# Output projections of four attention layers: seven block products, a bias on the scalar engine, and one batch of x kept in DRAM

## The chip, the core and the metric

The kernel runs on one core of a Trainium2 chip. It is one launch, and the metric is the device time of that launch in microseconds (us), as the median of three runs. A separate execution was recorded by the hardware profiler; all rows below come from it. Engines are named as in the profile: PE is TensorE (matrix products), PEld its weight loads, DVE is VectorE, ACT is ScalarE, POOL is GpSimd, and SP is the engine whose queue issues the DMAs. [...]

## The reference

Four layers in float32, one after the other, on `x` of 4 batches, 512 channels and 1024 positions. Every layer adds its result to `x`. Cut to what matters:

```python
# layer 0: attention with 8 heads of 64; layer 3: the same with 4 heads of 128, on group-normalised x
qkv = xs @ Wp.T + bp
attn = softmax(q @ k.T * SCALE)
res = attn @ v                      # heads side by side: 512 channels
out = res @ Wo.T + bo + xs          # the output projection, and x added

# layer 1: linear attention without a softmax, x + gamma * wval
# layer 2: attention with one head of 512 on layer-normalised x, x + out
```

## The kernel before

Channels are split into `NC` = 4 chunks of 128, so a batch of x is a tile of 128 partitions, 4 chunks and 1024 positions: 16 KB in each partition, 2 MB in all. The four batches stay in on-chip memory for the whole program (`xs`, line 559). Positions are split into two blocks of `TB` = 512. Layers 0 and 1 are interleaved: the linear attention of batch b - 1 (layer 1) is cut into `pieces`, which are put between the products of the query, key and value projection of batch b (layer 0). Then layer 2 runs over all batches, then layer 3. `plain_path` is the path that is timed. A general path behind it runs only when the largest sums of exponentials pass a limit.

**Seven products.** `seven_products` (line 685 to 800) computes a product of two-by-two blocks with seven block products and some additions in place of eight. The block sums of inputs are made by VectorE (`sum_inputs`, lines 665 to 668, four passes), those of weights by GpSimd (`sum_weights`, lines 673 to 676). The projections of queries, keys and values use it with 512 moving columns (L685) or 256 (`weights_moving`, L801). Before the change the output projection does not.

**Attention** (`attention`, for layers 0 and 3) is a loop over steps: two blocks of queries (`qb`), four groups of channels (`g`), and 8 steps of keys in layer 0 (a group there is a pair of heads) or 4 in layer 3. A step issues `scores` (products into one of two score buffers, an exponential of 128x1024 on ScalarE at L891, and a running sum on VectorE at L895 and L898) and, two steps later, `values` (L910 or L925). After a group's last step `sum_rows` sums the exponentials over partitions on TensorE (L937 or L945), VectorE takes the reciprocal (L657), and `normalise` (L954) multiplies the group's result into its chunk of `ot`. The exponentials have four buffers.

**The output projection** (`project_out`) of a block of queries needs all four chunks of `ot`. It is put on the list `later` with a count, and `tick`, called in every step, lets it run when the count is spent: in layer 0 five steps after its block's last one, in layer 3 three. The second block's projection falls into the next batch's query and key projection, where `seven_products` calls what is left on the list after its sixth call. It is 16 products of 128x512 (L969), and VectorE then adds result and bias to x:

```python
xv = x[:, o, bass.ts(qb, TB)]
nc.vector.scalar_tensor_tensor(xv, ps, bo[:, o : o + 1], xv, ALU.add, ALU.add)   # L958
```

In layer 3 each of the results then goes to the output by a DMA. The last block of the whole program has a projection of its own (`end_program`, L982 and L989).

**PSUM.** Products accumulate in `acc` tiles of 512 columns (`ps_acc`, 4 of them, a bank each) and score tiles of two banks (`ps_sc`, 2). In layer 0 a running group holds two `acc` tiles, one for each half of the partitions of the keys; in layer 3 it holds one.

**Order.** TensorE's instructions stay in the order in which the code issues them (`tc.manual_schedule`). Those of the other engines are ordered by a scheduler when the program is built, and `tc.issue_after` pins a few.

Of the kernel before, what the change touches and what calls it, by code (L numbers as in the profile page):

```python
# [13 lines left out]
F32 = mybir.dt.float32  # L14
# [460 lines left out]
def plain_path(ctx: ExitStack, tc: tile.TileContext, d: dict, out: bass.AP, count):  # L475
# [6 lines left out]

    nc = tc.nc

    const = ctx.enter_context(tc.tile_pool(name="const", bufs=1))
# [2 lines left out]
    work = ctx.enter_context(tc.tile_pool(name="work", bufs=1))  # L490
    small = ctx.enter_context(tc.tile_pool(name="small", bufs=2))
    PSUM = bass.MemoryType.PSUM
    ps_acc = ctx.enter_context(tc.tile_pool(name="ps_acc", bufs=4, space=PSUM))
    ps_sc = ctx.enter_context(tc.tile_pool(name="ps_sc", bufs=2, space=PSUM))

    def acc_tile():
        return ps_acc.tile([P, TB], F32, tag="acc", name="acc")
# [58 lines left out]
            nc.vector.tensor_tensor(bo, bo, cols[:, COL[name] : COL[name] + NC], ALU.add)  # L556
        return bo

    xs = [xpool.tile([P, NC, S], F32, tag=f"x{b}", name=f"x{b}") for b in range(B)]
# [5 lines left out]
    wview = d["wqkv0"].rearrange("(c p) o -> p c o", p=P)  # L565
    for c in range(NC):
        nc.sync.dma_start(xs[0][:, c, :TB], xin[0, :, c, :TB])
        nc.sync.dma_start(wqkv0[:, c, :C], wview[:, c, :C])
# [120 lines left out]
    def seven_products(  # L689
        n, weights, inputs, bias, dst, sums, ws=None, matmul=tokens_moving, view=lambda ps: ps,  # L690
        slots=0, first=False, done=lambda tb, o: None,
    ):

        stt = nc.vector.scalar_tensor_tensor
        one, five, seven, made = {}, {}, {}, {}
        inner = lambda o: block_sums(lambda i, j: weights(i, j, o))

        def mult(o, ps, w, x, start=True, stop=True, ms=(0, 1)):
            for m in ms:
                matmul(ps, w, x, m, o, start and m == 0, stop and m == 1)

        def join(out, ps, i, o, other):

            if bias is None:
                nc.vector.tensor_tensor(out, view(ps), other, ALU.add)  # L714
            else:
                joined[:] = [stt(out, view(ps), bias(i, o), other, ALU.add, ALU.add).ins]

        def p1(o, ms=(0, 1)):
            if 0 in ms:
                one[o] = acc_tile()  # L720
            mult(o, one[o], weights(0, 0, o), inputs(0, 0), stop=False, ms=ms)
            if 1 in ms:
                nc.scalar.copy(dst(0, 1, o), view(one[o]))

        def p2(o, ms=(0, 1)):
            mult(o, one[o], weights(0, 1, o), inputs(1, 0), start=False, ms=ms)
            if 1 in ms and bias is None:
                nc.scalar.copy(dst(0, 0, o), view(one.pop(o)))
            elif 1 in ms:
                nc.scalar.activation(dst(0, 0, o), one.pop(o), AF.Identity, bias=bias(0, o))  # L730

        def p3(o):
            mult(o, five[o], made[o][3], inputs(1, 1), start=False)
# [24 lines left out]
        if first:  # L758
            for f in (p1, p2):
                for m in range(2):  # L760
                    for o in range(n):
                        f(o, (m,))
            for o in range(2):
                made[o] = inner(o)
            t = sums()
        else:
            calls = [(p1, 0), (p1, 1), (p2, 0), (p2, 1)]
            if n > 2:
                calls += [(p1, 2), (p1, 3), (p2, 2), (p2, 3)]
# [88 lines left out]
        project_v(vt, wv, inputs, made, room())  # L858
        return q, k

    def attention(b, q, key, v, heads, scale, wo, bo, hooks={}, last=False, end=None):

# [86 lines left out]
        def normalise(qb, g):  # L949
            rd = rds.pop((qb, g))  # L950
            if g == 0 and not pair:
                ots[qb] = chunks_tile("ot", "ot")
            o = ots[qb][:, g, :]
            nc.vector.tensor_tensor(o, o if pair else outs.pop((qb, g))[0], rd, ALU.mult)  # L954

        def finish(qb, o, ps):
            xv = x[:, o, bass.ts(qb, TB)]
            nc.vector.scalar_tensor_tensor(xv, ps, bo[:, o : o + 1], xv, ALU.add, ALU.add)  # L958
            if last:
                nc.sync.dma_start(xout[b, :, o, bass.ts(qb, TB)], xv)  # L960

        def project_out(qb):
            ot = ots.pop(qb)

            for a in range(0, NC, 2):
                two = {o: acc_tile() for o in (a, a + 1)}
                for cs in (range(NC - 1), (NC - 1,)):
                    for o, c in itertools.product(two, cs):
                        nc.tensor.matmul(  # L969
                            two[o], lhsT=wo[:, c, bass.ts(o, P)], rhs=ot[:, c, :],  # L970
                            start=(c == 0), stop=(c == NC - 1),
                        )
                for o, ps in two.items():
                    finish(qb, o, ps)
# [24 lines left out]
        for m in range(0, len(steps) + 2, per):  # L999
# [3 lines left out]
            for n in range(m, m + per):  # L1003
                if n >= 2:
# [11 lines left out]
                    if n - 2 == len(steps) - 1 and end is not None:  # L1016
                        flush()
                        end_program(qb)
                    elif final and g == NC - 1:
# [341 lines left out]
    with tc.manual_schedule(engines={mybir.EngineType.PE}):  # L1361
# [8 lines left out]
        for b in range(B):  # L1370
# [12 lines left out]
            attention(b, q, lambda c, j: k[:, c, bass.ts(j, P)], vt, 8, 64.0**-0.5, wo0, bo0[0])  # L1383

# [59 lines left out]
        for b in range(B):  # L1444
# [28 lines left out]
            if b == 0:  # L1473

                query_sums()
            if b + 1 < B:
                norms = [layer_norm(b + 1, tb, after) for tb in range(NTB)]
                (add0, *n0), (add1, *n1) = norms
# [5 lines left out]
            else:  # L1484
# [29 lines left out]
        for b in range(B):  # L1514
# [6 lines left out]
            )  # L1521
            if b == 0:
                wo3 = load_wo(d["wo3"])
            flush()
            hooks = {}
            if b + 1 < B:
                ready = {}
# [2 lines left out]
                        lambda tb=tb, ready=ready: group_normed(b + 1, tb, ready)  # L1530
                    )
            attention(
                b, q, lambda c, j: k[:, c, bass.ts(j, P)], vt, 4, 128.0**-0.5, wo3, bo3, hooks,
                True, verdict if b == B - 1 else None,
            )

# [66 lines left out]
```

## Time and profile before

| quantity | value |
|---|---|
| median of 3 runs | 2527.16 us (2525.58 to 2527.5) |
| the profiled execution's own time | 2526.19 us |
| its span | 2524.3 us |
| mean granted TensorE clock | 0.999 |
| ScalarE busy | 657.2 us, 26% of the span |
| GpSimd busy | 239.0 us, 9% |
| L969, output projections: records, busy | 480, 211.7 us |
| L958, result and bias added to x: count, mean | 60, 751 ns |
| L898, running sum in attention: count, mean | 256, 1224 ns |
| L657, reciprocals in layers 0 and 3: count, mean | 64, 3358 and 3353 ns |
| one load of a whole batch of x, 2 MB: median from issue to landing | 20.8 us (three queued together) |

How to read it: the span is the profiled execution from its first to its last instruction, and its own time is 1.9 us more. A row of a timeline has its start, its length, the engine, the line of the kernel, the operation, output and input with shapes, and how many instructions it joins; in brackets stands the idle time of the engine just before it, and what ended that. A float32 matrix product leaves two records. The busy times of overlapping matrix products are modelled, so their lengths are better read from the chain of waits, where a row has start, length and the number of records.

### The profile page before, as it was taken

Reading aid. Unit: us, or ns where it says so; the run is one execution under the profiler, and the core shown is the slowest. Engines: PE = TensorE matmul, PEld = TensorE weight load, DVE = VectorE, ACT = ScalarE, POOL = GpSimd, SP = SyncE. Lnnn points to the kernel's source line nnn. Section 1 sums busy time; section 2 is a strip of 40 time slices with the busy share of each in tenths; the row PEclk is TensorE's granted clock in tenths of the full one; section 3 lists DMA queues with packets and bytes.
Section 4 is the critical chain, followed back from the end, with each engine's and each line's share of the span. In section 5 each row is a group of like instructions: output and inputs, shape, how many; then the busy total and the mean of one; then the engine's idle time right before and its main releaser. Section 6 shows DMA issues by size and latency. Waiting matters only on the chain.

```text
span 2524.3 us, 23992 instructions
## 1 busy us (share of the span) xinstructions
PE 2508.8 (99%) x9930; PEld 1245.0 (49%) x9930; DVE 1530.1 (61%) x1689; ACT 657.2 (26%) x781; POOL 239.0 (9%) x232
## 2 busy tenths in 40 slices
PE   9999999999999999999999999999999999999999
PEld 4544544454445444644646446445446445544643
DVE  3787588658865888657374563635643663654455
ACT  1443154315431643121110201012211220221121
POOL 3001100110020002002103011020010001002000
PEclk9999999999999999999999999999999999999999
DMA  6000000000000101000000000100000000000000
GB/s 246 1 1 1 5 1 1 1 5 1 1 1 14 50 9 42 5 1 0 0 1 1 0 4 1 67 0 17 17 17 1 0 17 17 1 17 17 1 13 22
DMA packets 17412, 38.87 MB, mean 15 GB/s; under 512 B 1552, under 2 KB 2064, under 8 KB 17296
## 3 DMA queue, kind: packets, MB, share of 16 engines
q1 hardware_dynamic: 17296, 37.26, 4.2%
q8 instruction: 80, 1.31, 0.2%
q14 instruction: 36, 0.29, 0.0%
HBM read 27.82 MB, written 8.39 MB: 14 GB/s over the span
## 4 chain that ended last, share of the span: by engine, by line
PE 98%; DVE 1%; DMA 0%; ACT 0%; issue 0%; SPq 0%; DVEq 0%; ACTq 0%
PE acc L685 19%; PE acc L801 12%; PE acc L1068 9%; PE acc L925 9%; PE sc L887 9%; PE acc L910 9%; PE sc L882 9%; PE acc L969 8%; PE acc L808 7%; PE acc L937 1%; PE acc L945 1%; PE feat L622 1%; PE acc L622 1%; PE acc L1160 1%; PE xt L1131 1%; PE upd L1226 1%
## 5 line engine op out<-in xcount | busy, mean ns | idle before, releaser
L891 ACT ACTIVATE pt<-sc 128x1024 f32<-128x1024 f32 x384 | 379.9, 1022 | 692.8 <-PE sc L887 408.5
L898 DVE TENSOR_TENSOR sum<-sum,pt 128x1024 f32<-128x1024 f32 x256 | 313.2, 1224 | 50.0 <-ACT pt L891 36.7
L910 PE MATMUL acc<-pt,v 64*64 64x512 f32 x2048 | 290.8, 590 | 0.0
L882 PE MATMUL sc<-q,k 64*64 64x512 f32 x2048 | 275.0, 590 | 1.1 <-ACT pt L891 1.1
L887 PE MATMUL sc<-q,k 128*128 128x512 f32 x512 | 240.0, 593 | 0.7 <-ACT pt L891 0.7
L925 PE MATMUL acc<-pt,v 128*128 128x512 f32 x512 | 239.9, 592 | 0.0
L969 PE MATMUL acc<-ot,wo 128*128 128x512 f32 x480 | 211.7, 595 | 0.8 <-DVE ot L954 0.8
L673 POOL TENSOR_TENSOR ws<-wqkv 128x256 f32<-128x256 f32 (+1 forms) x40 | 40.8, 1020 | 1417.4 <-PE acc L937 550.3
L657 DVE RECIPROCAL rd<-acc 128x512 f32<-128x512 f32 x32 | 107.5, 3358 | 109.7 <-PE acc L945 109.7
L685 PE MATMUL acc<-t,ws 128*128 128x512 f32 x384 | 173.9, 593 | 0.0
L1068 PE MATMUL acc<-pt,v 128*128 128x512 f32 x384 | 170.2, 592 | 0.0
L910 PEld LDWEIGHTS acc<-pt,v 64*64 64x64 f32 x2048 | 110.9, 133 | 112.7 <-issue 77.3
L882 PEld LDWEIGHTS sc<-q,k 64*64 64x64 f32 x2048 | 107.2, 133 | 116.0 <-issue 75.0
L925 PEld LDWEIGHTS acc<-pt,v 128*128 128x128 f32 x512 | 97.3, 190 | 122.5 <-issue 121.5
L887 PEld LDWEIGHTS sc<-q,k 128*128 128x128 f32 x512 | 96.7, 190 | 119.0 <-issue 97.5
L969 PEld LDWEIGHTS acc<-ot,wo 128*128 128x128 f32 x480 | 90.0, 190 | 120.6 <-issue 110.6
L958 DVE SCALAR_TENSOR_TENSOR x<-acc,bo,x 128x512 f32<-128x512 f32 x60 | 45.1, 751 | 146.5 <-PE acc L969 143.3
L1068 PEld LDWEIGHTS acc<-pt,v 128*128 128x128 f32 x384 | 72.8, 190 | 90.9 <-issue 89.2
L685 PEld LDWEIGHTS acc<-t,ws 128*128 128x128 f32 x384 | 72.5, 190 | 89.2 <-issue 87.5
L657 DVE RECIPROCAL rd<-rs 128x512 f32<-128x512 f32 x32 | 107.3, 3353 | 1.1
L895 DVE TENSOR_TENSOR sum<-pt 128x1024 f32<-128x1024 f32 x64 | 76.5, 1196 | 45.7 <-ACT pt L891 45.7
L714 DVE TENSOR_TENSOR v<-acc,v 128x512 f32<-128x512 f32 x72 | 49.7, 691 | 65.9 <-PE acc L801 65.7
(252 smaller groups left out, 3144.9 us busy)
## 6 DMA issues: line engine op xcount, KB each, us to landing
out<-x SPq DMA_DIRECT2D x32, 256.0 KB, 2.0
x<-in_x SPq DMA_DIRECT2D x3, 2048.0 KB, 20.8
wo<-in_wo SPq DMA_DIRECT2D x3, 1024.0 KB, 5.1
w<-in_w SPq DMA_DIRECT2D x1, 3072.0 KB, 11.1
wqkv<-in_wqkv SPq DMA_DIRECT2D x1, 3072.0 KB, 10.1
wqkv<-in_wqkv SPq DMA_DIRECT2D x2, 1024.0 KB, 10.0
x<-in_x SPq DMA_DIRECT2D x4, 256.0 KB, 4.9
wqkv<-in_wqkv SPq DMA_DIRECT2D x4, 256.0 KB, 5.4
```

The source lines that it names most:

```text
L657: nc.vector.reciprocal(rd, ps)
L685: nc.tensor.matmul(ps, lhsT=w[:, m, :], rhs=x[:, m, :], start=start, stop=stop, skip_group_check=True)
L801: nc.tensor.matmul(ps[:, bass.ts(r, C // 2)], lhsT=x[:, m, bass.ts(2 * o + r, P)], rhs=w[:, m, :], start=(start and r == 0), stop=stop, sk ...
L808: nc.tensor.matmul(ps, lhsT=x[:, m, bass.ts(o, P)], rhs=w[:, m, :], start=start, stop=stop, skip_group_check=True,)
L882: nc.tensor.matmul(ps[half(h), s, :], lhsT=key(g, i)[half(s), half(h)], rhs=q[qb][half(s), g, :], start=True, stop=True,)
L887: nc.tensor.matmul(ps[:, s, :], lhsT=key(g, 2 * i + s), rhs=q[qb][:, g, :], start=True, stop=True)
L891: nc.scalar.activation(pt, ps, AF.Exp, scale=scale)
L898: nc.vector.tensor_tensor(acc, acc, pt, ALU.add)
L910: nc.tensor.matmul(outs[qb, g][r][half(s), :], lhsT=v[i // 2][half(r), i % 2, g * P + s * hd : g * P + (s + 1) * hd], rhs=pt[half(r), s, : ...
L925: nc.tensor.matmul(outs[qb, g][0], lhsT=v[j // 2][:, j % 2, bass.ts(g, P)], rhs=pt[:, s, :], start=(j == 0), stop=(j == NT - 1),)
L969: nc.tensor.matmul(two[o], lhsT=wo[:, c, bass.ts(o, P)], rhs=ot[:, c, :], start=(c == 0), stop=(c == NC - 1),)
L1068: nc.tensor.matmul(out, lhsT=v[j // 2][:, j % 2, bass.ts(m, P)], rhs=pts[j][:, qb, :], start=(i == 0), stop=(i == NT - 1),)
```

## The change

It has four parts.

1. The output projections of layers 0 and 3 use seven products of blocks: two blocks of 256 channels on either side, two blocks of 256 positions. A product is four matrix products of 128x256, so a projection has 28 of these. It is issued in two halves: `lead` (the first block product, a copy of it to `d` on ScalarE, and the input sums on VectorE), one step earlier than the old projection, and `rest` (six block products and nine additions on VectorE), at the old place. Weight sums `os` are made once a layer on GpSimd. In layer 0 the last block of the last batch keeps the old form (`plain`), and so does the last block of the program.
2. The bias is added to x by ScalarE when a group is normalised in the code's order, so the projection's own additions no longer have it.
3. Three of four batches of x have a tile on chip. `away` writes a batch to DRAM, `back` reads one; both are DMAs on SP's queue, of 2 MB each. There are eight of each, and the first load of batch 3 from the input also moves to such a place. They stand after the value projection of layer 0's batches 1 to 3, at the start of layer 2, after each batch of layer 2, and in layer 3's batch 1.
4. The freed 16 KB a partition hold `os` (8 KB), `ou` (4 KB) and `oi` (6 KB).

The changed program's order on VectorE around a projection in layer 0's attention is: normalise of group 2, then a running sum, `t[0]`, three running sums, and so on to the normalise of group 4; then a running sum, `t[1]`, a running sum, `t[2]`, `t[3]`, two running sums, and then the nine additions of `rest`.

```diff
+    def away(b):
+        homes[b] = dram.tile([P, NC, S], F32, tag=f"home{b}", bufs=1, name=f"home{b}")
+        nc.sync.dma_start(homes[b], xs.pop(b))
+
+    def back(b):
+        nc.sync.dma_start(x_tile(b), homes.pop(b))
...
-    for b in range(1, B):
-        nc.sync.dma_start(xs[b], xin[b])
+    for b in range(1, B - 1):
+        nc.sync.dma_start(x_tile(b), xin[b])
...
+                if i == 4 and later:
+                    later.pop(0)[1]()
                 if i == min(5, len(calls) - 1):
                     t = sums()
                     while later:
...
             nc.vector.tensor_tensor(o, o if pair else outs.pop((qb, g))[0], rd, ALU.mult)
+            xv = x[:, g, bass.ts(qb, TB)]
+            nc.scalar.activation(xv, xv, AF.Identity, bias=bo[:, g : g + 1])
...
-            nc.vector.scalar_tensor_tensor(xv, ps, bo[:, o : o + 1], xv, ALU.add, ALU.add)
+            nc.vector.tensor_tensor(xv, ps, xv, ALU.add)
...
+            def mult(i, w, t, start=True, stop=True):
+                if start:
+                    ps[i] = acc_tile()
+                for m, o in itertools.product(range(2), range(2)):
+                    nc.tensor.matmul(
+                        ps[i][:, bass.ts(o, n)], lhsT=w[:, m, bass.ts(o, P)], rhs=t[:, m, :],
+                        start=(start and m + o == 0), stop=(stop and m == 1), skip_group_check=True,
+                    )
+
+            def add(i, out, *others):
+
+                for a in (view(ps[i]), *others):
+                    nc.vector.tensor_tensor(out, out, a, ALU.add)
...
+            def lead():
+                mult(1, w(0, 0), inputs(0, 0), stop=False)
+                nc.scalar.copy(d, view(ps[1]))
+                sum_inputs(t, inputs)
+
+            def rest():
+                mult(1, w(0, 1), inputs(1, 0), start=False)
+                finish(0, 0, 1, xv(0, 0))
+                mult(6, os[1], t[1])
+                add(6, d)
+                mult(7, os[2], t[2], stop=False)
+                nc.vector.tensor_tensor(e, d, view(ps[7]), ALU.add)
+                mult(5, os[0], t[0], stop=False)
+                finish(1, 1, 5, xv(1, 1), e)
+                mult(7, w(1, 1), t[3], start=False)
+                finish(1, 0, 7, xv(1, 0), d)
+                mult(5, os[3], inputs(1, 1), start=False)
+                finish(0, 1, 5, xv(0, 1), d)
...
                     elif final and g == NC - 1:
-                        later.append([2 * per + 1, lambda qb=qb: project_out(qb)])
+                        halves = []
+                        later.append([2 * per, lambda qb=qb, p=halves: start_out(qb, p)])
+                        later.append([2 * per + 1, lambda p=halves: p[1]()])
...
             flush()
+            if b > 0:
+                away(b - 1)
+                if b == 1:
+                    nc.sync.dma_start(x_tile(B - 1), xin[B - 1])
+                else:
+                    back(b - 2)
+            if b == 0:
+                os = output_sums(wo0)
...
+                away(B - 1)
+                back(2)
...
+            away(b)
+            back((b + 3) % B)
...
+                os = output_sums(wo3)
             flush()
+            if b == 1:
+                xs.pop(0)
+                back(B - 1)
```

`finish` here is `add` and, in layer 3, a DMA of that block to the output.

More of the change, by code (lines that the diff above doesn't have):

```diff
@@ L492, in plain_path @@
     PSUM = bass.MemoryType.PSUM
+    dram = ctx.enter_context(tc.tile_pool(name="dram", bufs=1, space=bass.MemoryType.DRAM))
     ps_acc = ctx.enter_context(tc.tile_pool(name="ps_acc", bufs=4, space=PSUM))
@@ L557, in weighted_bias, with x_tile @@
         return bo
-    xs = [xpool.tile([P, NC, S], F32, tag=f"x{b}", name=f"x{b}") for b in range(B)]
+    xs, homes = {}, {}
+    def x_tile(b):
+        xs[b] = xpool.tile([P, NC, S], F32, tag="x", bufs=B - 1, name=f"x{b}")
+        return xs[b]
+    def away(b):
[3 more added lines that the diff above has]
+        nc.sync.dma_start(x_tile(b), homes.pop(b))
     xin = d["x"].rearrange("b (c p) s -> b p c s", p=P)
@@ L565, in plain_path @@
     wview = d["wqkv0"].rearrange("(c p) o -> p c o", p=P)
+    x_tile(0)
     for c in range(NC):
@@ L859, in project_qkv, with output_sums, attention @@
         return q, k
-    def attention(b, q, key, v, heads, scale, wo, bo, hooks={}, last=False, end=None):
+    def output_sums(wo):
+        t = work.tile([P, 4, NC // 2, C // 2], F32, tag="os", bufs=1, name="os")
+        return sum_weights(
+            [t[:, i] for i in range(4)],
+            lambda i, j: wo[:, 2 * j : 2 * j + 2, i * C // 2 : (i + 1) * C // 2],
+        )
+    def attention(b, q, key, v, heads, scale, wo, os, bo, hooks={}, last=False, end=None, plain=False):
         hd = C // heads
@@ L962, in project_out @@
         def project_out(qb):
+            n = TB // 2
+            ot = ots.pop(qb)
+            w = lambda i, j: wo[:, 2 * j : 2 * j + 2, i * C // 2 : (i + 1) * C // 2]
+            inputs = lambda j, tb: ot[:, 2 * j : 2 * j + 2, bass.ts(tb, n)]
+            xv = lambda i, tb: x[:, 2 * i : 2 * i + 2, qb * TB + tb * n : qb * TB + (tb + 1) * n]
+            view = lambda ps: ps.rearrange("p (o t) -> p o t", o=2)
+            two = work.tile([P, 2, TB], F32, tag="ou", bufs=1, name="ou")
+            d, e = (view(two[:, i, :]) for i in range(2))
@@ new lines, in project_out @@
+            t = work.tile([P, 3, 2, n], F32, tag="oi", bufs=1, name="oi")
+            t = [t[:, i] for i in range(3)] + [inputs(0, 1)]
+            ps = {}
+            def mult(i, w, t, start=True, stop=True):
[5 more added lines that the diff above has]
+                        start=(start and m + o == 0), stop=(stop and m == 1), skip_group_check=True,
+                    )
@@ new lines, in add, with finish @@
+            def add(i, out, *others):
+                for a in (view(ps[i]), *others):
+                    nc.vector.tensor_tensor(out, out, a, ALU.add)
+            def finish(i, tb, *args):
+                add(*args)
+                if last:
+                    nc.sync.dma_start(
+                        xout[b, :, 2 * i : 2 * i + 2, qb * TB + tb * n : qb * TB + (tb + 1) * n],
+                        xv(i, tb),
+                    )
+            def lead():
+                mult(1, w(0, 0), inputs(0, 0), stop=False)
+                nc.scalar.copy(d, view(ps[1]))
+                sum_inputs(t, inputs)
@@ L963, in project_out, with start_out, project_out_plain @@
+            return lead, rest
+        def start_out(qb, halves):
+            halves.extend(project_out(qb))
+            halves[0]()
+        def project_out_plain(qb):
             ot = ots.pop(qb)
@@ L1018, in attention @@
                         end_program(qb)
+                    elif final and g == NC - 1 and plain and qb == NTB - 1:
+                        later.append([2 * per + 1, lambda qb=qb: project_out_plain(qb)])
                     elif final and g == NC - 1:
-                        later.append([2 * per + 1, lambda qb=qb: project_out(qb)])
+                        halves = []
+                        later.append([2 * per, lambda qb=qb, p=halves: start_out(qb, p)])
+                        later.append([2 * per + 1, lambda p=halves: p[1]()])
                 if parts:
@@ L1382, in plain_path @@
                 nc.sync.dma_start(w2, d["w2"].rearrange("(c p) o -> p c o", p=P))
-            attention(b, q, lambda c, j: k[:, c, bass.ts(j, P)], vt, 8, 64.0**-0.5, wo0, bo0[0])
+            attention(
+                b, q, lambda c, j: k[:, c, bass.ts(j, P)], vt, 8, 64.0**-0.5, wo0, os, bo0[0],
+                plain=(b == B - 1),
+            )
         def normed_tiles(b):
@@ L1532, in plain_path @@
             attention(
-                b, q, lambda c, j: k[:, c, bass.ts(j, P)], vt, 4, 128.0**-0.5, wo3, bo3, hooks,
+                b, q, lambda c, j: k[:, c, bass.ts(j, P)], vt, 4, 128.0**-0.5, wo3, os, bo3, hooks,
                 True, verdict if b == B - 1 else None,
```

## The prediction, made before the changed kernel ran

> **What bounds the kernel now.** I read the page's busy times, then the chain of waits, the groups by line and shape, and the timelines of the places that the change touches.
>
> ```profile
> PE 2508.8 (99%) x9930; PEld 1245.0 (49%) x9930; DVE 1530.1 (61%) x1689; ACT 657.2 (26%) x781; POOL 239.0 (9%) x232
> PE 98%; DVE 1%; DMA 0%; ACT 0%; issue 0%; SPq 0%; DVEq 0%; ACTq 0%
> ```
>
> TensorE (PE) is the bound over the whole. But 61% of VectorE (DVE) is an average over stages. In layer 0's attention:
>
> ```profile
> 133.89 0.63 DVE L659 TENSOR_REDUCE tops<-rs 128x1 f32<-128x512 f32 x1
> 134.44 0.67 DVE L660 TENSOR_REDUCE tops<-rd 128x1 f32<-128x512 f32 x1
> 135.02 0.68 DVE L954 TENSOR_TENSOR ot<-ot,rd 128x512 f32<-128x512 f32 x1
> 135.62 5.21 DVE L898 TENSOR_TENSOR sum<-sum,pt 128x1024 f32<-128x1024 f32 x4
> 140.74 1.22 DVE L895 TENSOR_TENSOR sum<-pt 128x1024 f32<-128x1024 f32 x1
> 141.88 0.68 DVE L921 TENSOR_TENSOR ot<-ot,acc 128x512 f32<-128x512 f32 x1
> 142.48 2.55 DVE L898 TENSOR_TENSOR sum<-sum,pt 128x1024 f32<-128x1024 f32 x2
> 144.94 0.68 DVE L943 TENSOR_TENSOR rs<-rs,acc 128x512 f32<-128x512 f32 x1
> 145.66 3.35 DVE L657 RECIPROCAL rd<-rs 128x512 f32<-128x512 f32 x1
> ...
> 150.06 0.68 DVE L954 TENSOR_TENSOR ot<-ot,rd 128x512 f32<-128x512 f32 x1
> 150.66 5.21 DVE L898 TENSOR_TENSOR sum<-sum,pt 128x1024 f32<-128x1024 f32 x4
> 156.81 1.61 DVE L958 SCALAR_TENSOR_TENSOR x<-acc,bo,x 128x512 f32<-128x512 f32 x2 [0.94 <-PE acc L969]
> 163.93 1.61 DVE L958 SCALAR_TENSOR_TENSOR x<-acc,bo,x 128x512 f32<-128x512 f32 x2 [5.51 <-PE acc L969]
> ```
>
> No idle time stands in brackets until 156.81: VectorE is full through a group of heads. Its reciprocals start 15.04 us apart (130.62, 145.66), while the group's matmuls are 128 records of 0.107 us (16 take 1.72 in the chain) plus 0.86 of row sums, 14.6. So here VectorE sets the pace by 0.44 us a group and catches up only while TensorE projects (5.51 us idle). The last rows hold the whole matter: four sums stand in VectorE's queue when the projection begins, and it does not care, since its first result comes 6 us later.
>
> [...]
>
> **The change part by part.** *TensorE's work.* Sixteen 128x512 products become 28 of 128x256; each product is two records.
>
> ```profile
> 55.02 24.17 PE acc L801 x112
> 224.00 13.99 PE acc L969 x32
> 397.21 14.18 PE acc L969 x32
> 1794.84 13.73 PE acc L969 x32
> 1863.51 13.99 PE acc L969 x32
> ```
>
> The x112 row is the same 256-wide shape: 24.17/112 = 0.216 us a record, so 56 records take 12.09 us, and one block product (8 records) 1.73. Before stood 13.73 to 14.18. Fourteen of the sixteen projections change, so the gain is 14 x 1.64 to 2.09, 23 to 29 us, if nothing waits. Then each place:
>
> *Layer 0, first query block (4 times).* VectorE's order in the changed program is: normalise, sum, t[1], sum, t[2], t[3], sum, sum, first addition to x. From 150.66: four sums 5.13 (the step between such rows, 135.62 to 140.74), three additions at 0.60 (150.06 to 150.66), the addition 0.68; it ends at 158.3. TensorE begins the second half at about 152 (it reached the projection at 150.5, and the first block product, 1.73, now comes before), does two block products, and wants a fifth accumulator at 155.5: of the four two hold the running group's values, one product 1, one product 6. Product 7 needs product 1's bank, free only after that addition: a wait of some 3 us. Four more block products (6.9) end at 165.2, against 164.68 now: +0.6. The early t[0] (0.60) is put between the sums of the third group, where VectorE sets the pace: +0.6. Together 4 x 1.2 = +4.7. Queued behind the waiting product are the next values and scores; nothing on ScalarE suffers first.
>
> *Layer 0, second query block (3 times; the last batch stays as it was).* It runs inside the next batch's projection. VectorE puts that batch's four input sums (223.32 on, step 1.19) between t's: 223.3 + 4.75 + 1.8 + 0.68 = 230.5. Two running projections hold two banks, so product 7 waits again, from 229.2 (224.0 and three block products); the end is 237.4 against 237.98: -0.5. Its t[0] costs 0.6 in VectorE-paced work as above. Together 3 x 0.1 = +0.2.
>
> *Layer 3 (4 and 3 times).* A group there costs VectorE 9.7 us (sums 1.16 + 2 x 1.22 + 0.69, reciprocal 3.36, reductions and product 3 x 0.68) of 14.6, and one running accumulator, not two, holds a bank in the first block, so product 7 needs no waiting. First block: 12.09 against 13.73, -1.64 x 4 = -6.6. Second block: VectorE has done the t's by 1863.3 (1856.5 + 4.75 + 1.8, rounded up), product 1 ends at 1867.0 (1863.5 and two block products), its addition at 1867.7, before product 7 at 1868.7; 12.09 against 13.99, -1.9 x 3 = -5.7. VectorE's 4 passes a projection become 13 (four t's, nine additions); the 9 more are 5.4 us at 0.60, hidden by the 8.15 + 5.26 us that it idles at 1792 to 1808.
>
> *Bias on ScalarE.* In layer 0 the input x itself is read by the value projection, so its last two bias passes wait for that projection's last product, and ScalarE then loads the exponential's table, which it now does 24 us early:
>
> ```profile
> 301.54 1.28 ACT L891 ACT_TABLE_LOAD   x1
> 326.92 1.94 ACT L891 ACTIVATE pt<-sc 128x1024 f32<-128x1024 f32 x2 [24.09 <-PE sc L882]
> ```
>
> The projection ends at 325.8; +0.2 to notice, two passes 1.2 (0.6 each from the 0.63 of a square from SBUF), load 1.28: the exponential starts at 328.5, not 326.92. Two score buffers fill, TensorE waits: +1.6 in batches 1 to 3. Batch 0 has no load: +0.4. Sum +5.2. Bounds: 0 if the passes run earlier than I read, +7 at 0.9 a pass. In layer 3 the projections read normalised copies, and the passes run in an attention's gaps (2.4 us idle before each exponential): 0, at most +1 a batch.
>
> *Weight sums on GpSimd.* Four passes of 1.26 (its 128x512 row, L674) fill the 4.96 us that its timeline shows idle from 27.8 in layer 0: 0, at most +0.5. In layer 3 it idles.
>
> *x in DRAM.* One load less at the start frees nothing that is waited for. The trips out and back are 2 MB. The rows for 1 MB and 3 MB (5.1 and 10.1 to 11.1 us) give 7.6 to 8.1 by interpolation;[...] I take 7.9. Most have 100 us. Two are short, because VectorE's statistics of that x stand in its queue among the joins of the query and key projection. Layer 3, batch 0: x3 is final at 1650.8, out and back end at about 1667; the statistics come at 1667. Batch 1: the outputs of x0 land at 1879, x3 is back at 1887, wanted at 1886.6. About 1.5 us of either is absorbed before TensorE runs out of banks. I take +0.5, with 0 to +10.
>
> *Sum.* 4.7 + 0.2 + 5.2 - 6.6 - 5.7 + 0.5 = -1.7. Against the profiled execution (2526.19 us; 2524.3 of it span) that is 2524.5; its median of three is 0.97 higher, so I predict 2525.5: layer 3 gains 12, layer 0 gives 10 back.
>
> **The rivals.** *Layer 0's starts are hidden* (the passes finish earlier, or its first group has slack): -6.9, 2520. For it: VectorE idles 2.4 us at that point; against: TensorE paces that group. *Layer 0 gains too*: were VectorE not late, its seven projections would give 7 x -1.65 = -11.5 in place of +4.9, so -18, 2509. For it speaks TensorE's 98% of the chain; against, the rows from 150.66. *The trip through DRAM is late* (slower): at 12 us for 2 MB, statistics of x2 block VectorE until 1675 (8 - 1.5 = +6.7), those of x3 until 1891 (+3.2): 2535; each further microsecond of transfer costs 3, and above 11 us the sign turns. For it: no row writes 2 MB out; against: the 3 MB rows. *Nothing is gained anywhere*, since 256-wide products run no faster per column: excluded by the x112 row.
>
> **How the numbers follow.** About 0.2% (5 us) is what a measurement of this kernel tells from no change: 2522.1 to 2532.2. Forecast 0.45, with its own range 2522 to 2531; starts hidden 0.22; layer 0 gaining 0.13; late trips 0.20. The second mostly counts as faster: faster 0.35, same 0.43, slower 0.22. The range reaches to 2512 (half of layer 0's gain) and 2535.
>
> **What would show it.** Product 7 in layer 0 waits about 3 us for an addition to x, 7 times with 1.5 in the later ones; none in layer 3. TensorE waits about 1.8 us for an exponential at each start of layer 0's batches 1 to 3. Attention groups in layer 0 stay 15.04 us apart, one in each block 0.6 longer. Statistics of x2 and x3 wait under 2 us for a DMA. A first addition that comes before the sums in layer 0 would prove me wrong by 10 us, a statistics wait of over 4 us by as much the other way.

## The result, and the profile after

The changed kernel takes 2520.39 us (median of 11 runs, 2519.57 to 2521.27) against 2526.67 us of the kernel before in the same series (11 runs, 2525.34 to 2527.5). The ratio is 0.9976, with an interval of 0.9966 to 0.9985: 6.3 us faster, 0.24%. The forecast was 2525.5 us. The time lies inside the range on record, 5 us below the forecast, and just beyond the bound that the prediction drew between faster and no change.

The page of the changed kernel first, its busy times and its chain of waits:

```profile
PE 2488.8 (99%) x10266; PEld 1287.7 (51%) x10266; DVE 1608.0 (64%) x1815; ACT 705.5 (28%) x859; POOL 254.8 (10%) x240
PE 94%; DVE 4%; ACT 1%; issue 1%; DMA 0%; SPq 0%; DVEq 0%; ACTq 0%
```

TensorE has 20.0 us less of busy time, but the span fell by 5.4 us only (2524.3 to 2518.9): 14.6 us have become waiting. The chain shows for whom, but not how long: VectorE's share went from 1% to 4%, and 3% of the span is 76 us, far more than was waited: behind each wait the chain follows the whole run of VectorE's instructions that led to it. What TensorE waits for, and for how long, is listed in the view of waits (total us, number of waits, longest):

```profile
PE acc L1012 <- DVE x L1020: 10.7, 7, 1.8
PE acc L701 <- DMA wqkv<-in_wqkv: 4.9, 1, 4.9
PE sc L908 <- ACT pt L917: 4.1, 4, 1.3
```

The first row is new: the seven projections of layer 0 (L1012) wait for an addition to x (L1020). The third had 1.1 us in the kernel before (4 waits, longest 0.3). These two, 10.7 and 3.0 more, are nearly all of the 14.6. "Product 7" and the like below are the numbers that `mult` has in `rest`.

To see where the time goes, one needs a clock that both kernels share. The 64 reciprocals of the two attention layers (L657 before, L673 after) stand in both timelines in the same order, one for each group. The difference of their starts, at the places where it moves:

| group of heads | before, us | after, us | after minus before |
|---|---|---|---|
| layer 0, batch 0, first block, group 1 | 100.54 | 101.42 | +0.88 |
| same, group 3 | 130.62 | 131.91 | +1.29 |
| second block, group 2 | 189.76 | 191.18 | +1.42 |
| same, group 3 | 204.80 | 206.63 | +1.83 |
| batch 1, first block, group 1 | 347.18 | 349.59 | +2.41 |
| same, group 3 | 377.26 | 380.08 | +2.82 |
| second block, group 1 | 421.01 | 424.31 | +3.30 |
| same, group 3 | 451.09 | 454.80 | +3.71 |
| batch 2, first block, group 1 | 593.47 | 597.76 | +4.29 |
| batch 3, first block, group 1 | 839.75 | 845.93 | +6.18 |
| batch 3, second block, group 4 | 961.10 | 968.15 | +7.05 |
| layer 3, batch 0, first block, group 1 | 1738.64 | 1745.45 | +6.81 |
| same, second block, group 1 | 1811.19 | 1816.35 | +5.16 |
| batch 1, first block, group 1 | 1955.78 | 1959.05 | +3.27 |
| batch 3, second block, group 4 | 2502.50 | 2497.03 | -5.47 |

At the end of layer 0 the changed kernel is 7.05 us late, of which 0.88 were there before any attention; layer 0 itself loses 6.2. Layer 2 loses nothing (-0.24 up to layer 3), and layer 3 gains 12.3. This column is called the ladder below. It has three kinds of steps in layer 0. Each third group of a block with the new projection loses 0.41 (seven times; the second block of batch 3, which keeps the old form, has no such step). Each first block's projection loses 0.48 (0.13 in batch 0). From the end of a second block to the next batch it is +0.58, and within that the new scores begin only 1.42 late in batch 1, where 1.83 stood before: the second block's projection gains 0.41, and the start of the batch loses 1.0. In layer 3 the third group of a first block is 1.4 us late in batches 0 to 2, and the fourth is back, so nothing is lost there.

The timeline of VectorE and TensorE around the first projection of layer 0:

```profile
150.76 0.67 DVE L676 TENSOR_REDUCE tops<-rd 128x1 f32<-128x512 f32 x1
151.35 0.68 DVE L980 TENSOR_TENSOR ot<-ot,rd 128x512 f32<-128x512 f32 x1
151.95 1.22 DVE L924 TENSOR_TENSOR sum<-sum,pt 128x1024 f32<-128x1024 f32 x1
153.08 0.69 DVE L682 TENSOR_TENSOR oi<-ot,oi 128x512 f32<-128x512 f32 x1
153.68 1.22 DVE L924 TENSOR_TENSOR sum<-sum,pt 128x1024 f32<-128x1024 f32 x1
154.82 0.69 DVE L683 TENSOR_TENSOR oi<-ot 128x512 f32<-128x512 f32 x1
155.54 0.69 DVE L684 TENSOR_TENSOR ot<-ot,oi 128x512 f32<-128x512 f32 x1
156.15 2.55 DVE L924 TENSOR_TENSOR sum<-sum,pt 128x1024 f32<-128x1024 f32 x2
158.62 0.68 DVE L1020 TENSOR_TENSOR x<-x,acc 128x512 f32<-128x512 f32 x1
159.21 0.68 DVE L1020 TENSOR_TENSOR ou<-ou,acc 128x512 f32<-128x512 f32 x1
161.38 0.69 DVE L1041 TENSOR_TENSOR ou<-ou,acc 128x512 f32<-128x512 f32 x1 [1.49 <-PE acc L1012]
```

```profile
159.35 3.72 PE L1012 MATMUL acc<-oi,os 128*128 128x256 f32 x16 [1.76 <-DVE x L1020]
```

TensorE asks for product 7's bank (one of the four `acc` tiles) at 157.6 (159.35 less 1.76). It gets it when the addition at 158.62 ends, and that stands behind four sums of exponentials and three input sums with no idle time between them. From there on it is VectorE that waits.

In layer 3 there is no such wait. Its chain of waits at a first block (start, length, records):

```profile
1798.22 1.73 PE acc L1012 x8
1799.95 1.72 PE sc L913 x4
1801.66 1.72 PE acc L951 x4
1803.38 10.36 PE acc L1012 x48
```

1.73 and 10.36 are 12.09 us for the projection, where 13.73 stood before.

A start of a batch of layer 0, ScalarE and then TensorE:

```profile
326.43 1.58 ACT L982 ACTIVATE x<-x,bo 128x512 f32<-128x512 f32 x2 [22.86 <-PE acc L819]
328.03 1.28 ACT L917 ACT_TABLE_LOAD   x1
329.32 1.94 ACT L917 ACTIVATE pt<-sc 128x1024 f32<-128x1024 f32 x2
```

```profile
327.18 1.95 PE L908 MATMUL sc<-q,k 64*64 64x512 f32 x16
330.40 2.00 PE L908 MATMUL sc<-q,k 64*64 64x512 f32 x16 [1.27 <-ACT pt L917]
```

Two bias passes and then the table load stand ahead of the first exponential. The scores wait 1.27 us for it, and waited 0.28 before. The chain of waits at the same place has only the second of the two passes behind the value projection, and so it is at the starts of batches 2 and 3:

```profile
323.60 3.67 PE acc L819 x16
327.29 0.72 ACT x L982
328.03 1.28 ACT L917
```

### The profile page after: what moved, and what is told of

Its sections match the earlier page's. It is cut to its first block, busy times and chain, and to the rows that moved or that the text cites. A ratio compares the mean times of both kernels' runs of the same rounds, so it can differ in the third digit from the quotient of the medians.

```text
span 2518.9 us, 24923 instructions
## 1 busy us (share of the span) xinstructions
PE 2488.8 (99%) x10266; PEld 1287.7 (51%) x10266; DVE 1608.0 (64%) x1815; ACT 705.5 (28%) x859; POOL 254.8 (10%) x240
## 4 chain that ended last, share of the span: by engine, by line
PE 94%; DVE 4%; ACT 1%; issue 1%; DMA 0%; SPq 0%; DVEq 0%; ACTq 0%
PE acc L701 18%; PE acc L819 12%; PE acc L1165 9%; PE acc L951 9%; PE sc L913 9%; PE acc L936 8%; PE sc L908 8%; PE acc L826 7%; PE acc L1012 5%; PE acc L963 1%; PE feat L638 1%; PE acc L971 1%; DVE rd L673 1%; DVE sum L924 1%; PE acc L638 1%; PE acc L1257 1%
## 5 line engine op out<-in xcount | busy, mean ns | idle before, releaser
L673 DVE RECIPROCAL rd<-acc 128x512 f32<-128x512 f32 x32 | 107.4, 3357 | 107.5 <-PE acc L971 107.5
L936 PEld LDWEIGHTS acc<-pt,v 64*64 64x64 f32 x2048 | 104.6, 133 | 122.5 <-issue 99.2
L908 PEld LDWEIGHTS sc<-q,k 64*64 64x64 f32 x2048 | 101.5, 133 | 127.5 <-issue 95.5
L673 DVE RECIPROCAL rd<-rs 128x512 f32<-128x512 f32 x32 | 107.3, 3353 | 1.1
L739 ACT COPY v<-acc 128x512 f32<-128x512 f32 x24 | 14.0, 584 | 273.4 <-PE acc L819 273.4
L819 PE MATMUL acc<-ws,t 128*128 128x256 f32 x384 | 87.3, 379 | 0.0
L1012 PE MATMUL acc<-oi,os 128*128 128x256 f32 x336 | 76.7, 381 | 10.7 <-DVE x L1020 10.7
```

The costliest lines, as they stand in the source:

```text
L673: nc.vector.reciprocal(rd, ps)
L819: nc.tensor.matmul(ps[:, bass.ts(r, C // 2)], lhsT=x[:, m, bass.ts(2 * o + r, P)], rhs=w[:, m, :], start=(start and r == 0), stop=stop, sk ...
L908: nc.tensor.matmul(ps[half(h), s, :], lhsT=key(g, i)[half(s), half(h)], rhs=q[qb][half(s), g, :], start=True, stop=True,)
L936: nc.tensor.matmul(outs[qb, g][r][half(s), :], lhsT=v[i // 2][half(r), i % 2, g * P + s * hd : g * P + (s + 1) * hd], rhs=pt[half(r), s, : ...
L1012: nc.tensor.matmul(ps[i][:, bass.ts(o, n)], lhsT=w[:, m, bass.ts(o, P)], rhs=t[:, m, :], start=(start and m + o == 0), stop=(stop and m == ...
```

## The experiments

All kernels start from the changed one, and all were timed in five rounds against the kernel before. Of each edit the lines that matter are shown; `...` marks what is left out.

**The new projection in layer 3 alone.** Layer 0 has its old projection, with the bias in VectorE's addition and without the weight sums on GpSimd:

```diff
-                    elif final and g == NC - 1 and plain and qb == NTB - 1:
+                    elif final and g == NC - 1 and pair:
                         later.append([2 * per + 1, lambda qb=qb: project_out_plain(qb)])
...
-            nc.scalar.activation(xv, xv, AF.Identity, bias=bo[:, g : g + 1])
+            if not pair:
+                nc.scalar.activation(xv, xv, AF.Identity, bias=bo[:, g : g + 1])
...
-            nc.vector.tensor_tensor(xv, ps, xv, ALU.add)
+            if pair:
+                nc.vector.scalar_tensor_tensor(xv, ps, bo[:, o : o + 1], xv, ALU.add, ALU.add)
+            else:
+                nc.vector.tensor_tensor(xv, ps, xv, ALU.add)
```

> The changed kernel with the seven products, and the bias on ScalarE, in layer 3 alone; layer 0 has its old projection with the bias in VectorE's addition; the trips of x through DRAM stay. My theory: layer 0 gives back about 7 us, by three costs that all belong to the change of the projection there (starts, t[0], product 7), and layer 3 gains 12.3. So this kernel ends 12 us below the kernel before, 6.5 below the changed one: about 2514.5, ratio 0.9952. Layer 2 then begins within 0.5 us of its place in the kernel before. Rival, the loss in layer 0 comes from the trips of x or the later load of weights and not from the projection: the time stays near the changed kernel's, 2520 (0.9976), and layer 2 begins 5 to 7 us late.

Measured: 2513.61 us against 2526.48, ratio 0.9949 (0.9935 to 0.9962). Layer 2's first reciprocal comes 0.79 us earlier than in the kernel before, where the changed kernel has it 7.05 late, and layer 3 then gains 12.3 as before. So the loss belongs to the projection and the bias in layer 0, with what they bring along, and not to the trips of x. The 0.9 us more than expected have two visible sources: the first loads (-0.42 at the first group), and -0.24 from each batch of layer 0 to the next (against them stands 0.35 lost at one group of batch 2). There the old projection stands one call earlier than in the kernel before, since the changed `seven_products` takes an entry of the list after its fifth call; the next run bears on it.

**Three tiles for x, and the old projections.** All projections and biases are the old ones, and the weight sums are gone. One thing beside the trips is left of the change: the earlier call just named.

```diff
-                        halves = []
-                        later.append([2 * per, lambda qb=qb, p=halves: start_out(qb, p)])
-                        later.append([2 * per + 1, lambda p=halves: p[1]()])
+                        later.append([2 * per + 1, lambda qb=qb: project_out_plain(qb)])
```

> The kernel before with one part of the change alone: three tiles for four batches of x, and the trips through DRAM at their places; all projections are the old 16 products and the bias is in VectorE's addition. My theory: nothing that is waited for is late, so 0 to +0.5 us against the kernel before (2526.7 to 2527.2), of which 0.3 come from the order of the first loads. Rival: trips are late in layer 3 or their traffic delays other loads: +3 to +8 us, with VectorE's statistics of x2 or x3 waiting for a DMA for several us.

Measured: 2525.45 us against 2526.48, ratio 0.9996 (0.9987 to 1.0004): no difference that this can tell. Its statistics wait for no trip. In the changed kernel, by the view of VectorE's waits, one does, and nothing in the ladder moves there. The second fence has the trips from the changed kernel's page (count, size, median us to landing), the third this kernel's projection of a second block, in layer 0 and in layer 3:

```profile
DVE st L1405 <- DMA x<-home: 0.8, 1, 0.8
```

```profile
home<-x SPq DMA_DIRECT2D x8, 2048.0 KB, 6.3
x<-home SPq DMA_DIRECT2D x8, 2048.0 KB, 7.8
```

```profile
221.47 13.73 PE acc L1061 x32
1860.56 13.73 PE acc L1061 x32
```

The kernel before has 13.99 us in both places. The ladder of this run falls by 0.24 or 0.25 behind each second block, in layer 0 and in layer 3. So these steps need neither seven products nor a bias on ScalarE. The earlier place of the projection is the only change in TensorE's order there, and TensorE waits for no trip; still, the place was not tried without the trips.

**Bias passes behind the exponentials.**

```diff
-            nc.scalar.activation(pt, ps, AF.Exp, scale=scale)
+            latest[:] = [nc.scalar.activation(pt, ps, AF.Exp, scale=scale).ins]
...
-            nc.scalar.activation(xv, xv, AF.Identity, bias=bo[:, g : g + 1])
+            with tc.issue_after(latest[0]) if pair else nullcontext():
+                nc.scalar.activation(xv, xv, AF.Identity, bias=bo[:, g : g + 1])
```

> The changed kernel with one pin more: in layer 0 each bias pass on ScalarE stands behind the last exponential that the code has issued before it, so none stands ahead of the first exponential of a batch. My theory: the passes and the table load behind them cost 0.6 us at the start of batch 0 and 1.0 us at each of the three others, 3.6 in all, and nothing elsewhere: about 3.6 below the changed kernel, 9 to 10 below the one before (2517, ratio 0.9962); TensorE's wait for the first exponential of batches 1 to 3 falls from 1.27 back to 0.28 us. Rival, the passes only move: inside attention each delays an exponential or the copy of a group's row sums by up to 0.7 us, and VectorE sets the pace there, so 32 passes cost up to 10 us: 2520 to 2527.

Measured: 2517.21 us against 2526.48, ratio 0.9963 (0.9949 to 0.9976). ScalarE and TensorE at the same start of batch 1:

```profile
302.17 1.28 ACT L918 ACT_TABLE_LOAD   x1
327.55 1.94 ACT L918 ACTIVATE pt<-sc 128x1024 f32<-128x1024 f32 x2 [24.09 <-PE sc L909]
```

```profile
328.62 2.00 PE L909 MATMUL sc<-q,k 64*64 64x512 f32 x16 [0.28 <-ACT pt L918]
```

The table is loaded 24 us ahead again, and the wait is 0.28. From one batch to the next the ladder is 1.0 us lower, three times, and its other steps are as they were (+0.41 and +0.48): the passes cost nothing inside attention. At batch 0 the expected 0.6 was not there to gain: TensorE waits 0.3 for its first exponential in the changed kernel as in the one before. The 0.8 us that this kernel is ahead there come earlier, from the first loads. The changed kernel and the seven of this study, all with the same order of first loads, have their first reciprocal between 0.81 us before and 0.88 us after that of the kernel before. So the +0.88 of the changed kernel's profile is most likely a difference between executions; without it the profile's -5.4 becomes -6.3, which is what the medians have.

**Input sums on GpSimd.** One part of VectorE's queue taken away in layer 0:

```diff
-                sum_inputs(t, inputs)
+                sum_inputs(t, inputs, nc.gpsimd if pair else nc.vector)
```

> The changed kernel with the four input sums of a projection in layer 0 made by GpSimd instead of VectorE; layer 3 keeps them on VectorE. My theory: product 7 waits for a bank that is free after the first addition to x, and that addition stands in VectorE's queue behind three of the sums (1.8 us); and t[0] lengthens a group that VectorE paces by 0.41. Without them: 7 x 0.41 = 2.9, the wait of 1.76 in each first block gone (4 x 1.8 = 7), that of 1.23 in each second block (3 x 1.2 = 3.7): 13 us below the changed kernel, 19 below the one before (2507.5, ratio 0.9925). Rival one, GpSimd at 1.26 us a pass is late for product 6 or 7 and the wait only changes its name: within 2 us of the changed kernel, 2520. Rival two, the wait is set by the sums of exponentials ahead of the additions, of which TensorE's own progress is the clock: some 3 us gained from t[0] alone, 2517.

Measured: 2541.43 us against 2526.48, ratio 1.0054 (1.0040 to 1.0067): slower by 15 us, which neither the theory nor a rival had. VectorE and GpSimd around the first projection:

```profile
151.61 7.85 DVE L924 TENSOR_TENSOR sum<-sum,pt 128x1024 f32<-128x1024 f32 x4
159.38 0.68 DVE L1020 TENSOR_TENSOR x<-x,acc 128x512 f32<-128x512 f32 x1
```

```profile
151.84 2.13 POOL L682 TENSOR_TENSOR oi<-ot,oi 128x512 f32<-128x512 f32 x1 [28.84 <-DVE ot L980]
153.93 2.24 POOL L683 TENSOR_TENSOR oi<-ot 128x512 f32<-128x512 f32 x1
156.25 2.12 POOL L684 TENSOR_TENSOR ot<-ot,oi 128x512 f32<-128x512 f32 x1
```

VectorE has three instructions fewer, yet its four sums take 7.85 us instead of 5.21 (136.57 to 141.78 in the same timeline, where GpSimd rests). GpSimd's passes take 2.1 to 2.2 us where its 128x512 pass over weights has 1.26 in the kernel before. The additions come later than before, and the wait of product 7 grows from 1.76 to 2.95 us (20.0 in all, from 10.7). So the two slow each other down while both run, by these numbers; by what means is not shown.

But the longer waits are not the whole loss. Here are TensorE's 16 records behind the wait, in the first block of batch 0 and in that of batch 1:

```profile
160.20 6.66 PE L1012 MATMUL acc<-oi,os 128*128 128x256 f32 x16 [2.95 <-DVE x L1020]
416.49 3.69 PE L1012 MATMUL acc<-oi,os 128*128 128x256 f32 x16 [2.95 <-DVE x L1020]
```

After the first of these waits TensorE's granted clock was 0.50 from 160 to 166 us; after the second it stayed at 1.00. It fell to 0.50 behind four of the seven waits, and the rows there take 9.1 us more than 3.69 each. The mean granted clock of this kernel's runs is 0.996 or 0.997, that of all other kernels here 0.999 or 1.000. Why it fell at four of the places and not at the others is not shown. Of the 21 us between this kernel and the changed one, then, 9 are a lower clock; an estimate without them (2541.43 less 9.1) is 2532, still slower than the kernel before.

The run doesn't refute the theory of the bank, but it doesn't test it either: the queue ahead of the addition became longer, and the wait with it.

**The banks given back by ScalarE.** VectorE's queue is left as it is, and only what the bank waits for is changed:

```diff
+            def clear(i, to):
+                if pair:
+                    nc.scalar.copy(to, view(ps[i]))
+                    early[i] = to
...
-                for a in (view(ps[i]), *others):
+                for a in (early.pop(i) if i in early else view(ps[i]), *others):
...
                 mult(1, w(0, 1), inputs(1, 0), start=False)
+                clear(1, e)
                 finish(0, 0, 1, xv(0, 0))
                 mult(6, os[1], t[1])
+                clear(6, t[1])
```

> The changed kernel with two copies more in each projection of layer 0: ScalarE copies the finished products 1 and 6 out of their banks (into e and into the tile of t[1], which are free then), and VectorE's additions read the copies. VectorE has as many instructions as in the changed kernel, in the same order. My theory: TensorE waits in layer 0's projections because the bank of product 1 is given back by an addition that stands behind three sums of exponentials and three input sums. With the copies the bank is free at 0.8 us after product 1, before product 7 wants it: the waits of 1.76 (four first blocks) and 1.23 us (three second blocks) go, 10.7 in all: 2509.5 to 2510, ratio 0.9933; 4.2 of layer 0's loss are left at its starts and 2.9 in t[0]. Rival, what limits is VectorE's whole amount of work in these stages, which is unchanged: TensorE waits as long at the next group's first exponentials or copies, and the time stays within 2 us of the changed kernel's, 2520.

Measured: 2508.57 us against 2526.13, ratio 0.9928 (0.9915 to 0.9942). ScalarE's two copies, VectorE's first addition and TensorE's products 6, 7 and 5 in one row:

```profile
154.82 0.59 ACT L1010 COPY ou<-acc 128x512 f32<-128x512 f32 x1 [1.67 <-PE acc L1017]
156.54 0.59 ACT L1010 COPY oi<-acc 128x512 f32<-128x512 f32 x1 [1.14 <-PE acc L1017]
```

```profile
157.54 0.68 DVE L1025 TENSOR_TENSOR x<-x,ou 128x512 f32<-128x512 f32 x1
```

```profile
154.62 5.34 PE L1017 MATMUL acc<-oi,os 128*128 128x256 f32 x24
```

The first addition still stands at the same place behind the same sums, and TensorE no longer cares: product 1 is out of its bank at 155.41, 0.79 us after the products behind it began (154.62), and 24 records run without a gap. The row of 10.7 us is gone from the waits. In the ladder each first block now gains 1.55 us in batches 1 to 3 where it lost 0.48, which is nearly the 1.65 that a first block gains in layer 3. The turn is 2.03 us in each first block and 1.49 in each second one, 12.6 in all, 1.9 more than the row of waits had; where these 1.9 lie is not shown. The number and the order of VectorE's instructions are unchanged, and its additions take 0.68 or 0.69 us as before, so it was the banks and not the work. The copies of product 1 and of product 6 were not tried apart.

**Both together**, the copies and the later bias passes:

> bank_copy with the bias passes of layer 0 behind the exponentials as well. Theory: the two gains add, as they lie in different places: 10.7 + 3.8 below the changed kernel, 2506, ratio 0.9918. If the later bias passes get into the way of the copies on ScalarE, less than 12 together.

Measured: 2505.58 us against 2526.13, ratio 0.9917 (0.9903 to 0.9930). The two gains add, within what can be told.

**And t[0] later.** The input sums in layer 0 are pinned behind the block's last normalise:

```diff
-                sum_inputs(t, inputs)
+                with tc.issue_after(normed[0]) if pair else nullcontext():
+                    sum_inputs(t, inputs)
```

> bank_late with t[0] in layer 0 pinned behind the normalise of the block's last group. Theory: t[0] then no longer lies in a group that VectorE paces (7 x 0.41 = 2.9 us gained), and in the projection, where no bank waits for VectorE any more, its 0.6 us are hidden, as t[1] is still made before product 6: 2503, ratio 0.9907. Rival, t[1] comes late for product 6 or the next group starts late by as much: no gain against bank_late.

Measured: 2504.87 us, ratio 0.9915 (0.9901 to 0.9928), not to be told from the kernel without the pin. The seven steps of 0.41 are gone from the ladder. But a first block now gains 0.96 where it gained 1.55, and TensorE has a new wait there:

```profile
160.58 1.99 PE L1020 MATMUL acc<-ot,wo 128*128 128x256 f32 x8 [0.31 <-DVE ou L1052]
```

The second half of product 7 is added onto the bank that VectorE must have read first, and that read (L1052, 159.83 to 160.52) is now 0.6 us later in the queue. The rival was right about the time, though it is product 7 and not product 6 that waits: what t[0] leaves in one place (7 x 0.41) it mostly takes in the other (4 x 0.59).

The two last kernels, at 2505.58 and 2504.87 us, are faster than both the kernel before and the changed one.

## Why the prediction was right or wrong

*That layer 3 gains and layer 0 gives back* was right, and the first of the two to the tenth: -6.6 and -5.7 were forecast, and the ladder has 4 x 1.65 = 6.6 and 3 x 1.90 = 5.7 us. No product waits there, as stated. But of the 1.90 of a second block only 1.65 belong to the shorter product. The other 0.25 the old projection gains too, with the trips and one call earlier (13.73 in place of 13.99). The forecast took the 13.99 from its row without asking why it is longer than 13.73, so there the number is right for a reason that is in part another.

*Layer 0's first blocks*, +4.7 (165.2 less 164.68 is 0.5 and not the 0.6 that was summed; 4.4 would follow): the wait for product 1's bank is there four times, in the place and for the reason given, and so is the loss of t[0] in a group that VectorE paces. Both were too large. The wait was put at 3 us and is 1.76: on the changed kernel's clock, 1.29 later, the bank was to be asked for at 156.8 and was asked for at 157.6, and the addition was to end at 159.6 and ended at 159.3. The end hardly notices who was late: 0.48 instead of 0.6. The step of t[0] was costed as its full 0.60, and is 0.41. Together the first blocks lost 4 x 0.41 + 3 x 0.48 + 0.13 = 3.2.

*Layer 0's second blocks*, +0.2: 3 x (0.41 - 0.41) = 0, with a wait of 1.23 where 1.5 was forecast. Of the gain of 0.41, 0.24 are the step that the old projection has here too.

*The starts*, +5.2: this is the term that failed. Three starts cost 1.0 each and not 1.6, and the one of batch 0 nothing, 3.0 in all; the pin that puts the passes behind the exponentials gives back the same 3.0. The prediction let both passes stand behind the value projection's last product: 0.2 us to notice (the kernel before has 0.20 from the start of one product at 300.74 to the copy of the product ahead of it at 300.94), 1.2 for two passes, 1.28 for the table. The first pass begins at 326.43, about 0.8 us before that product ends (323.60 and 3.67 are 327.27), seemingly because a pass needs only its own chunk of x to have been read. Only the second follows it: 0.02 in the chain from the product's end to the pass, 0.72 for one pass, 1.28 for the table and some hundredths between, 2.05 in all and not 2.68. A pass took longer than the 0.6 that was estimated, 0.71 in the median of 64 (L982) against 0.63 for the square of the same shape (L1278), which made up for a part of the error. The lower bound that the prediction set, "if the passes run earlier than I read", was the right doubt.

*x in DRAM*, +0.5: nothing can be told, as the run with the trips and the old projections shows. The wait of 0.8 us on one trip is within "under 2 us", and the size of 7.9 us was right for the way back (7.8).

*The sum.* Forecast -1.7 on the profile, seen -5.4. Of the difference, 2.2 us are the starts, 1.5 the first blocks, 0.2 the second and 0.5 the trips, 4.4 together; 0.2 more came before layer 3; against them stand the 0.9 of the first loads in the profiled execution. The errors were small and all on one side: each of the four costs came out smaller than forecast, the trips within what can be told.

*The rivals.* The time fell on the number of "layer 0's starts are hidden" (2520), but that is chance, and not what happened: the starts cost 3.0 us. "Layer 0 gains too" didn't happen in this change; the copies by ScalarE, which take VectorE's lateness out of the way of the banks, show that its size was right: in the ladder of that run the seven projections gain 6.6 and 5.7 us, 12.3 against the 11.5 of the rival (0.7 of it is the step of 0.24 three times), though t[0] still takes 2.9 of it. "Late trips" is excluded. "Nothing is gained anywhere" was excluded by the right row but argued badly: a column costs the same in both shapes (0.84 ns in a record: 112 records of 256 columns take 24.17 us, 32 of 512 take 13.73), and the gain is that 28 products of 256 columns have fewer of them (7168) than 16 of 512 (8192).

## What to carry to other kernels

A shorter product was worth its saving only where the accumulators came free as fast as it wanted them: 1.65 us a first block in layer 3, where nothing waited, and a loss of up to 0.48 in layer 0, where product 7 waited 1.76. So look up which engine gives back each bank, and what stands ahead of that instruction in its queue. A copy by an engine that idles (ScalarE was busy for 28% of the span) can give a bank back early, although it is work added: it took the 10.7 us of waits away. Moving work from VectorE to GpSimd cost both of them here, 7.85 us for four sums in place of 5.21 and 2.1 to 2.2 for a pass in place of 1.26. When a kernel comes out slower than its waits explain, look at the granted clock of each stretch: here it was 9 us of a loss of 21. Where many small costs are summed, ask of each how much of it lies beside something else, and carry the doubt as a range of the sum: here three terms, and perhaps a fourth, erred to the same side.

## What the runs showed of the hardware

With GpSimd making the input sums of the projection, VectorE's sums and GpSimd's passes stretched each other. In a second block, where the two alternated, three of VectorE's four 128x1024 input sums took 2.17 to 2.28 us, and the first, begun 0.16 us ahead of GpSimd's first pass, 1.22; GpSimd's passes took 2.13 to 2.25, where its pass of this shape over weights had 1.26 in the kernel before:

```profile
230.66 2.17 DVE L682 TENSOR_TENSOR t<-x,t 128x1024 f32<-128x1024 f32 x1
232.76 2.28 DVE L683 TENSOR_TENSOR t<-x 128x1024 f32<-128x1024 f32 x1
```

```profile
229.57 2.18 POOL L682 TENSOR_TENSOR oi<-ot,oi 128x512 f32<-128x512 f32 x1 [3.51 <-DVE ot L980]
231.72 2.25 POOL L683 TENSOR_TENSOR oi<-ot 128x512 f32<-128x512 f32 x1
```

Each of these lasts nearly as long as 1.22 and 1.26 together (2.48), so the two engines did little more than one.

In the same kernel TensorE's granted clock fell to 0.50 after four of its seven waits of 2.73 to 2.95 us, for some 3 to 7 us each: 16 records then took 5.26 to 6.66 us in place of 3.69. After the waits of 1.76 and 1.23 us at the same places of the changed kernel it stayed at 1.00, and the rows take 3.72. Three of the waits of 2.73 to 2.95 us had no such fall, so no threshold can be read from these runs.
